# PSUM copies moved to ScalarE, a mask step moved to GpSimd, and a new order of TensorE's units in a four-layer graph network

## The chip, the cores and the metric

The kernel runs on one core of one Trainium2 chip. The metric is the device time of one execution in microseconds (us). Kernels are compared by the median of several executions, and a profile comes from one further execution, which has its own time. TensorE (PE in the profile) does the matrix products and the transposes, PEld is its loading of weights, VectorE is DVE, ScalarE is ACT, GpSimd is POOL, and SP issues the DMAs.

## What is computed

There are 32 graphs of 512 nodes with 256 features, each with a 512 by 512 adjacency matrix of zeros and ones. Four layers follow one another, each of them attention over the neighbours, and each ends in a sum with its own input and a layer norm:

```
x = norm(x + L0(x, adj))  # 4 heads of 64, relu, sum, norm per head
x = norm(x + L1(x, adj))  # one head, relu logits, elu
x = norm(x + L2(x, adj))  # 8 heads of 32, symmetric mask, then feed forward 1024
x = norm(x + L3(x, adj))  # one head, leaky relu logits
```

Layer 3 has logits f_i + g_j and, where they are negative, 0.2 times that; the softmax over the neighbours weighs the rows of h W. The kernel writes the numerator as max(exp(-0.8 f_i), exp(0.8 g_j)) times a factor exp(0.2 g_j), which is multiplied into the row j of the values, so that one vector instruction per tile makes the attention weights.

## The kernel before, in words

**Tiles.** A tile has 128 partitions; a graph has R = 4 row tiles and K = 2 column tiles. Every graph passes through ten steps: `edges` (the transposed adjacency is loaded in two halves and turned into bytes by ScalarE), `x`, `layer 0`, `layer 1`, `mask` (the adjacency is loaded and joined with its transpose, `symmetric`, line 378), `qkv`, `attention`, `projection`, `feed forward`, `layer 3`.

**Units and places.** Each step is a Python generator, cut by `yield` into units: for example `h0p` has one unit per row tile. `paced` (line 111) gives a unit a place, which is 12054 (`PERIOD`) times the graph's number plus a figure of the table `PLACES` (line 28). `heapq.merge` over the 32 graphs takes the unit with the lowest place next; where a unit's place lies below that of the unit just done, it follows at once. The order so made is TensorE's order, kept as it is (`manual_schedule`, line 798 and following). The instructions of the other engines are put in order by the tile framework, which lets ready instructions go ahead but mostly keeps the order in which they were written. So about four and a half graphs are under way together, and in the steady state each stretch of one period holds every unit once, of different graphs.

**Units by name.** The profile names TensorE's work by its result: h0p, gp, o (half tiles, `pt,hv`), den and backp for layer 0; xt1p, h1p, gp, o (`h,pt`) for layer 1; xt2p, qkp, vp for `qkv`; s, cp and den (`pr,ones`) for attention; wop for the projection; ytp, f1p, f2p for feed forward; xt3p, h3p, gp, o (`h,pt`) for layer 3. Line 104 is the helper that records all products. In this text gp0, gp1 and gp3 are the `gp` of the three layers, o0/2 is the unit of layer 0's product for j = 2 with its `den` matmuls, and s/c1j3h0 is a score unit of attention (half c, tile j, pair of heads h).

**Layer 0's products.** For each j of 4, VectorE makes four tiles `pt` (one per head, `kept`, line 394, instruction on line 397) out of `gb` (line 349), which TensorE multiplies in the unit o0/j. The `gb` and `pt` tiles, with others of the first layers, come from one ring of 9 buffers:

```python
        return buf([P, N], "part", name, {"a": 9, "c": 6}[stage[0]])
```

All four `gb` tiles are live until the last j, and `pt` tiles come free when the `den` matmuls of their j are done.

**The copies.** `evacuate` (line 304) gives a copy out of PSUM to VectorE for odd i and to ScalarE for even i; `transposed` (line 310) uses it for the two halves of each transposed matrix (xt1, xt2, xt3, yt), and layer 0 uses it for its three results `back`. `project` (line 323) copies each h tile by ScalarE. In layer 3 three exponentials (lines 711 to 713) then read all rows at once, and VectorE scales the values (line 714).

**The mask's diagonal.** `symmetric` takes the maximum of both directions on VectorE (line 388), sets the diagonal by a maximum with a small identity (line 390), and turns the last row tile into `shut` (line 391).

Of the kernel before, what the change touches and what calls it, by code (L numbers as in the profile page):

```python
# [14 lines left out]
ALU = mybir.AluOpType  # L15
# [10 lines left out]

PERIOD = 12054
PLACES = {
    "edges": [-5445, -1601, -916, 215],
    "x": [5461],  # L30
    "mask": [15415, 16243, 18300, 20727],
    "layer 0": [
        -31803, -31803, -30970, -28094, 618, 969, 969, 969, 8266, 10068, 10166, 10897,
        11770, 12293, 12293,
    ],
    "layer 1": [15146, 15174, 15397, 15397, 15397, 16015, 16537, 16946, 17233, 17233, 17233, 17233],
    "qkv": [19264, 19264, 22129, 22143, 22914, 23775, 24075, 24348, 24348, 24686, 25270],
    "attention": [
        -649, -498, -422, 1139, 26271, 26286, 26286, 26286, 26339, 26457, 26496, 27188,
        27431, 27452, 28958, 28958, 28979, 28979, 29061, 30394, 32151, 32151, 33609, 33609,  # L40
    ],
    "projection": [34273, 34335, 34335, 34355, 34984],
    "feed forward": [
        35875, 35881, 36402, 37091, 38264, 38376, 38376, 38428, 38428, 38589, 38589, 39322,
        39483, 39517, 39599, 40391, 41034, 41340, 41342,
    ],
    "layer 3": [44176, 44176, 45119, 45119, 45119, 46223, 46369, 47123, 47123, 47952, 47999, 48256],
}
STAGES = {"edges": "a", "x": "a", "layer 0": "a", "layer 1": "a", "feed forward": "c", "layer 3": "c"}
ALL = mybir.DependencyInfo(mybir.DependencyClass.Sync, mybir.DependencyReason.DATA)  # L50
# [22 lines left out]
def fast_path(ctx: ExitStack, tc: tile.TileContext, a: dict, out: bass.AP, bad: bass.AP):  # L73
# [230 lines left out]
    def evacuate(i, dst, src):  # L304
        if i % 2:
            nc.vector.tensor_copy(dst, src)
        else:
            nc.scalar.copy(dst, src)

    def transposed(y, name):  # L310

        t = buf([P, K, N], "xt", name, 1)
        for k in range(K):
            yield
            p = bank(name + "p")
            for r in range(R):
                product(nc.tensor.transpose,
                    p[:, r * P : (r + 1) * P], y[r][:, k * P : (k + 1) * P], ident
                )
            evacuate(k, t[:, k, :], p)  # L320
        return t

    def project(xt, w, cols, name):

        h = buf([P, R, cols], "h", name, {"a": 2}.get(stage[0], 1))
        for r in range(R):
            yield
            p = bank(name + "p")
            for k in range(K):
                product(nc.tensor.matmul,  # L330
                    p[:, :cols],
                    xt[:, k, r * P : (r + 1) * P],
                    w[:, k, :cols],
                    start=k == 0,
                    stop=k == K - 1,
                )
            nc.scalar.copy(h[:, r, :], p[:, :cols])
        return h
# [39 lines left out]
    def symmetric(b, at):  # L378

        a2 = sb.tile([P, R - 1, N], U8, tag="a2", name="a2", bufs=1)  # L380
        shut = sb.tile([P, N], BF16, tag="shut", name="shut", bufs=1)
        parts = [a2[:, r, :] for r in range(R - 1)] + [shut]
        for h in range(2):
            yield
            t = half(b, "adj", h)
            yield
            for r in range(h * R // 2, (h + 1) * R // 2):
                in_place(nc.vector.tensor_max(parts[r], at[:, r, :], t[:, r % (R // 2), :]))
                diag = parts[r][:, r * P : (r + 1) * P]
                nc.vector.tensor_max(diag, diag, identb)  # L390
        nc.vector.tensor_scalar(shut, shut, 0.0, SHUT, op0=ALU.is_equal, op1=ALU.mult)
        return a2, shut

# [7 lines left out]
    def layer0(x, xt, at, rd, mv, var):  # L401
        h = yield from project(xt, w0, D + 2 * H, "h0")
        values = hv[:, :, :, :HO]
        nc.vector.tensor_add(
            values,
            h[:, :, :D].rearrange("p r (h e) -> p r h e", h=H),
            bias0.rearrange("p (h e) -> p h e", h=H).unsqueeze(1).to_broadcast([P, R, H, HO]),
        )
        ex = buf([P, 2, H, R], "ex", "ex0", 2)
        s, d = h[:, :, D : D + H], h[:, :, D + H :]  # L410
        nc.scalar.activation(ex[:, 0], s.rearrange("p r h -> p h r"), AF.Exp, scale=-0.99)
        nc.scalar.activation(ex[:, 1], d.rearrange("p r h -> p h r"), AF.Exp, scale=0.99)
        nc.scalar.activation(hv[:, :, :, HO], d, AF.Exp, scale=0.01)
        nc.vector.tensor_mul(values, values, hv[:, :, :, HO:].to_broadcast([P, R, H, HO]))
        gbs = []
        for hh in range(H):
            gbs.append((yield from along(ex[:, 0, hh, :].unsqueeze(2), "gb0")))
        den, *ops = (bank(name) for name in ("den0", "o0", "o0"))
        for j in range(R):
            pt = [kept("pt0", gbs[hh], at[:, j, :], ex[:, 1, hh, j : j + 1]) for hh in range(H)]  # L420
            yield
            for hh in range(H):
                product(nc.tensor.matmul,
                    ops[hh // 2][hh % 2 * HO : (hh % 2 + 1) * HO, :],
                    hv[:, j, hh, :HO],
                    pt[hh],
                    start=j == 0,
                    stop=j == R - 1,
                )
            for hh in range(H):  # L430
                product(nc.tensor.matmul,
                    den[hh * DH : (hh + 1) * DH, :],
                    hv[:, j, hh, HC - DH :],
                    pt[hh],
                    start=j == 0,
                    stop=j == R - 1,
                )
        back = []
        for i, o in enumerate((den, *ops)):
            t = part("back")  # L440
            evacuate(i, t, o)
            back.append(t)
        y = sb.tile([P, R, D], F32, tag="y", name="y0", bufs=3)
        for i in range(1 + H // 2):
            yield
            p = bank("backp")
            for r in range(R):
                product(nc.tensor.transpose,
                    p[:, r * P : (r + 1) * P], back[i][:, r * P : (r + 1) * P], ident
                )  # L450
            if i == 0:
                rdh = rd.rearrange("p (i r h) -> p i r h", i=H // 2, r=R)
                for i in range(H // 2):
                    nc.vector.reciprocal(
                        rdh[:, i],
                        p.rearrange("p (r h e) -> p r h e", r=R, h=H)[
                            :, :, 2 * i : 2 * i + 2, DH - 1
                        ],
                    )
                continue  # L460
            nc.vector.scalar_tensor_tensor(
                y[:, :, (i - 1) * P : i * P].rearrange("p r (h e) -> p r h e", h=2),
                p.rearrange("p (r h e) -> p r h e", r=R, h=2),
                0.0,
                rdh[:, i - 1].unsqueeze(3).to_broadcast([P, R, 2, HO]),
                op0=ALU.max,
                op1=ALU.mult,
            )
        nc.vector.tensor_add(x, x, all_rows(bet0))
        nc.vector.tensor_add(y, y, h[:, :, :D])  # L470
        head_layernorm(y, 1e-6, var)
        nc.vector.tensor_mul(y, y, all_rows(gam0))
        nc.vector.tensor_add(y, y, x)
        layernorm(y, 1e-5, mv[0])
        return y
# [229 lines left out]

    def layer3(x, at, rd, mv):
        xt = yield from transposed([x[:, r, :] for r in range(R)], "xt3")
        h = yield from project(xt, w3g, D + 2, "h3")
        ex = buf([P, 2, R, 1], "ex", "ex3", 2)
        f, g = h[:, :, D : D + 1], h[:, :, D + 1 :]  # L710
        nc.scalar.activation(ex[:, 0], f, AF.Exp, scale=-0.8)
        nc.scalar.activation(ex[:, 1], g, AF.Exp, scale=0.8)
        nc.scalar.activation(f, g, AF.Exp, scale=0.2)
        nc.vector.tensor_mul(h[:, :, :D], h[:, :, :D], f.to_broadcast([P, R, D]))
        gb = yield from along(ex[:, 0], "gb3")
        pt = [kept("pt3", gb, at[:, j, :], ex[:, 1, j, :]) for j in range(R)]
        for r in range(R):
            p = yield from attend(pt, h, r, "o3")
            nc.vector.reciprocal(rd[:, r : r + 1], p[:, D : D + 1])
            nc.vector.scalar_tensor_tensor(  # L720
                x[:, r, :], p[:, :D], rd[:, r : r + 1], x[:, r, :], op0=ALU.mult, op1=ALU.add
            )
        layernorm(x, 1e-5, mv[5])
        return x
# [736 lines left out]
```

## Time and profile before

| | |
|---|---|
| median of 3 runs | 3603.0 us (3601.5 to 3603.07) |
| the profiled execution | 3604.45 us, of which 3602.7 us are its span (first to last instruction) |
| PE, PEld | 3460.6 us and 2344.0 us busy |
| DVE, ACT, POOL | 3036.6, 2083.5 and 5.2 us busy |
| granted TensorE clock, mean | 0.987 |

How to read it: a group line gives the source line, the engine, the instruction with output and input tiles, its count, busy time, the mean duration of one, and the idle time before it with what ended that. A timeline line gives the start in us from the span's start, the duration of a merged piece, and in brackets the idle time ahead of it. Busy time of PE overlaps for neighbouring matmuls, so lines of one group can sum to more than the page's busy time; where a matmul waits in the pipeline, its record gets longer. A windows line gives the stretch, its length, and the busy us and number of instructions of each engine in it.

### The profile page before, as it was taken

The page shows a single profiled execution, that of the slowest core. Times are in us where ns is not written, and L with a number is a line of the kernel's source. Part 1 is how long each engine was busy: PE and PEld are TensorE (multiplying, and loading weights), DVE is VectorE, ACT ScalarE, POOL GpSimd, SP SyncE. Part 2 cuts the span into 40 slices and gives each one's busy share as a digit, 9 for nine tenths or more (in the row PEclk, how much of TensorE's full clock was granted, in tenths as well). Part 3 has the DMA queues.
Part 4 walks back from the last instruction along what each step waited for, and adds up shares of the span by engine and source line. Part 5 has one row for each costly group of instructions (what it writes and reads, how often), then busy time and mean ns, then how long its engine had stood idle before and what let it go on. Part 6 is the DMA issues. An engine that isn't in the chain of part 4 may idle for free.

```text
span 3602.7 us, 48721 instructions
## 1 busy us (share of the span) xinstructions
PE 3460.6 (96%) x17224; PEld 2344.0 (65%) x17318; DVE 3036.6 (84%) x5498; ACT 2083.5 (58%) x4993; POOL 5.2 (0%) x43
## 2 busy tenths in 40 slices
PE   6899999999999999999999999999999999999986
PEld 3466666766666766666776666776666776666655
DVE  5779888889888889888888888888988888988763
ACT  3556656656656655656655556655656655655542
POOL 0000000000000000000000000000000000000000
PEclk8999999999999999999999999999999999999998
DMA  4333332334332234333234332233323233323120
GB/s 127 82 74 88 66 75 66 70 77 88 68 76 65 68 77 88 71 74 68 65 77 88 75 71 70 61 77 88 82 64 71 60 76 88 88 58 66 36 53 13
DMA packets 164027, 260.85 MB, mean 72 GB/s; under 512 B 20416, under 2 KB 56384, under 8 KB 163776
## 3 DMA queue, kind: packets, MB, share of 16 engines
q1 hardware_dynamic: 163776, 257.65, 32.5%
q8 instruction: 140, 2.29, 0.3%
q14 instruction: 111, 0.91, 0.1%
HBM read 106.57 MB, written 16.78 MB: 34 GB/s over the span
## 4 chain that ended last, share of the span: by engine, by line
PE 90%; ACT 5%; DVE 3%; issue 1%; DMA 0%; SPq 0%; DVEq 0%; ACTq 0%
PE o L104 19%; PE f2p L104 12%; PE f1p L104 12%; PE s L104 7%; PE cp L104 7%; PE qkp L104 6%; PE den L104 5%; PE h3p L104 3%; PE h1p L104 3%; PE wop L104 3%; PE h0p L104 3%; PE vp L104 3%; ACT y L280 2%; PE gp L104 1%; ACT gb L349 1%; PE backp L104 1%
## 5 line engine op out<-in xcount | busy, mean ns | idle before, releaser
L397 DVE SCALAR_TENSOR_TENSOR pt<-gb,ex,at 128x512 f32<-128x512 f32 x768 | 526.5, 750 | 198.5 <-ACT gb L349 158.0
L611 ACT ACTIVATE pr<-s 128x512 f32<-128x512 f32 x1024 | 551.2, 612 | 32.4 <-PE s L104 16.4
L614 DVE TENSOR_TENSOR pr<-pr,a 128x1024 f32<-128x1024 f32 x384 | 459.8, 1218 | 38.4 <-ACT pr L611 38.4
L104 PE MATMUL f2p<-wf,ft 128*128 128x256 f32 x2048 | 485.3, 380 | 6.7 <-ACT ft L684 6.6
L104 PE MATMUL f1p<-yt,wf 128*128 128x256 f32 x2048 | 484.0, 379 | 0.0
L641 DVE TENSOR_TENSOR pr<-pr 128x1024 f32<-128x1024 f32 x384 | 453.6, 1218 | 31.6 <-PE cp L104 28.1
L104 PE MATMUL o<-h,pt 128*128 128x257 f32 x2048 | 474.2, 384 | 3.2 <-DVE pt L397 3.2
L104 PEld LDWEIGHTS o<-h,pt 128*128 128x128 f32 x2048 | 386.9, 192 | 83.5 <-DVE mvs L274 23.5
L104 PEld LDWEIGHTS f2p<-wf,ft 128*128 128x128 f32 x2048 | 385.1, 190 | 63.5 <-ACT ft L684 11.4
L104 PEld LDWEIGHTS f1p<-yt,wf 128*128 128x128 f32 x2048 | 387.1, 190 | 52.1 <-DVE lo L537 0.3
L280 ACT ACTIVATE y<-y,rs 128x256 f32<-128x256 f32 x768 | 398.5, 597 | 14.8 <-DVE rs L276 14.8
L684 ACT ACTIVATE ft<-f1p,cols 128x256 f32<-128x256 f32 x512 | 215.1, 473 | 311.9 <-PE f1p L104 311.9
L104 PE MATMUL s<-qk 128*128 128x512 f32 x1024 | 367.7, 465 | 3.7 <-DMA qk<-lo 2.4
L273 DVE BATCH_NORM_STATS2 bn<-y 128x6 f32<-128x256 f32 x768 | 296.1, 411 | 4.4
L104 PE MATMUL cp<-pr,v 128*32 128x512 f32 x2048 | 269.4, 609 | 5.5 <-DVE pr L614 3.7
L104 PE MATMUL o<-pt,hv 128*64 128x512 f32 x1024 | 264.7, 612 | 4.6 <-DVE pt L397 4.6
L104 PEld LDWEIGHTS s<-qk 128*128 128x128 f32 x1024 | 187.5, 191 | 109.3 <-issue 77.9
L104 PE MATMUL qkp<-xt,wqkv 128*128 128x512 f32 x512 | 240.8, 603 | 0.0
L349 ACT COPY gb<-gp 128x512 f32<-128x512 f32 x192 | 110.5, 581 | 167.4 <-PE gp L104 167.4
L104 PEld LDWEIGHTS o<-pt,hv 128*64 128x64 f32 x1024 | 69.9, 137 | 159.6 <-issue 83.2
L536 ACT ACTIVATE hi<-qkp,cols 128x512 fp32r<-128x512 f32 x128 | 87.9, 686 | 138.5 <-PE qkp L104 138.5
L104 PEld LDWEIGHTS qkp<-xt,wqkv 128*128 128x128 f32 x512 | 94.9, 191 | 108.8 <-issue 103.7
(145 smaller groups left out, 4615.6 us busy)
## 6 DMA issues: line engine op xcount, KB each, us to landing
qk<-hi SPq DMA_DIRECT2D x512, 128.0 KB, 3.4
qk<-lo SPq DMA_DIRECT2D x512, 128.0 KB, 4.0
adjt<-in_adjt SPq DMA_DIRECT2D x64, 512.0 KB, 3.8
adj<-in_adj SPq DMA_DIRECT2D x64, 512.0 KB, 3.8
xt<-in_xt SPq DMA_DIRECT2D x32, 512.0 KB, 3.6
x<-in_x SPq DMA_DIRECT2D x32, 512.0 KB, 6.4
out<-y SPq DMA_DIRECT2D x32, 512.0 KB, 4.9
wf<-in_w1t SPq DMA_DIRECT2D x1, 1024.0 KB, 8.0
```

The source lines that it names most:

```text
L104: latest[0] = what(*args, **kwargs).ins.name
L273: nc.vector.bn_stats(st[:, r, :], y[:, r, :])
L280: nc.scalar.activation(y[:, r, :], y[:, r, :], AF.Identity, bias=rs[:, 1, r : r + 1], scale=rs[:, 0, r : r + 1],)
L349: nc.scalar.copy(g, p)
L397: nc.vector.scalar_tensor_tensor(t, g, f, edges, op0=ALU.max, op1=ALU.mult)
L536: nc.scalar.activation(hi, p, AF.Identity, bias=bias)
L611: nc.scalar.activation(t[:, i, :], s, AF.Exp, scale=QSCALE)
L614: nc.vector.tensor_mul(t, t, edges)
L641: nc.vector.tensor_add(t, t, u)
L684: nc.scalar.activation(ft[:, f, :], p[:, f, :], AF.Relu, bias=bf1[:, ff + f : ff + f + 1])
```

## The change

Five edits, with all places given anew.

1. `transposed` copies both halves by ScalarE.
2. Layer 0 copies all three `back` tiles by ScalarE.
3. The diagonal of the mask is set by GpSimd: a selection with a fill value, on bytes for three row tiles and on bf16 for the fourth.
4. Layer 3 no longer calls `project`: each h3p tile is followed by three exponentials on one column of PSUM and a ScalarE copy scaled by one of them; the vector multiplication of line 714 is gone.
5. The table `PLACES` is new; `PERIOD` is not.

```diff
 PLACES = {
-    "edges": [-5445, -1601, -916, 215],
-    "x": [5461],
-    "mask": [15415, 16243, 18300, 20727],
+    "edges": [-3978, -1691, -957, 174],
+    "x": [5375],
+    "mask": [15529, 15550, 17375, 20858],
     "layer 0": [
-        -31803, -31803, -30970, -28094, 618, 969, 969, 969, 8266, 10068, 10166, 10897,
-        11770, 12293, 12293,
+        -32810, -32810, -32810, -32129, 5406, 5406, 5406, 5452, 8379, 10181, 10354, 11030,
+        12979, 12979, 12979,
     ],
-    "layer 1": [15146, 15174, 15397, 15397, 15397, 16015, 16537, 16946, 17233, 17233, 17233, 17233],
-    "qkv": [19264, 19264, 22129, 22143, 22914, 23775, 24075, 24348, 24348, 24686, 25270],
+    "layer 1": [15397, 15397, 15551, 15551, 15637, 16368, 16395, 17082, 17350, 17359, 17359, 17361],
+    "qkv": [17440, 17444, 22256, 22270, 23119, 23902, 25371, 25371, 25371, 25371, 25371],
     "attention": [
-        -649, -498, -422, 1139, 26271, 26286, 26286, 26286, 26339, 26457, 26496, 27188,
-        27431, 27452, 28958, 28958, 28979, 28979, 29061, 30394, 32151, 32151, 33609, 33609,
+        -2905, -2905, -2905, -1865, 26410, 26425, 26425, 26425, 26478, 26596, 27423, 27447,
+        27455, 27460, 28382, 28382, 28780, 28780, 29468, 30180, 32292, 32292, 33750, 33750,
     ],
-    "projection": [34273, 34335, 34335, 34355, 34984],
+    "projection": [34383, 34383, 34383, 34383, 35158],
...
-    "layer 3": [44176, 44176, 45119, 45119, 45119, 46223, 46369, 47123, 47123, 47952, 47999, 48256],
+    "layer 3": [44306, 44306, 45121, 45121, 46359, 46359, 46477, 48020, 48020, 48023, 48398, 48528],
 }
...
-            evacuate(k, t[:, k, :], p)
+            nc.scalar.copy(t[:, k, :], p)
...
                 diag = parts[r][:, r * P : (r + 1) * P]
-                nc.vector.tensor_max(diag, diag, identb)
+                if r < R - 1:
+                    diag = diag.bitcast(mybir.dt.int8)
+                nc.gpsimd.affine_select(
+                    diag,
+                    diag,
+                    pattern=[[-1, P]],
+                    compare_op=ALU.not_equal,
+                    fill=1.0,
+                    base=0,
+                    channel_multiplier=1,
+                )
...
             t = part("back")
-            evacuate(i, t, o)
+            nc.scalar.copy(t, o)
...
-        h = yield from project(xt, w3g, D + 2, "h3")
+        h = buf([P, R, D + 2], "h", "h3", 1)
         ex = buf([P, 2, R, 1], "ex", "ex3", 2)
-        f, g = h[:, :, D : D + 1], h[:, :, D + 1 :]
-        nc.scalar.activation(ex[:, 0], f, AF.Exp, scale=-0.8)
-        nc.scalar.activation(ex[:, 1], g, AF.Exp, scale=0.8)
-        nc.scalar.activation(f, g, AF.Exp, scale=0.2)
-        nc.vector.tensor_mul(h[:, :, :D], h[:, :, :D], f.to_broadcast([P, R, D]))
+        for r in range(R):
+            yield
+            p = bank("h3p")
+            for k in range(K):
+                product(nc.tensor.matmul,
+                    p[:, : D + 2],
+                    xt[:, k, r * P : (r + 1) * P],
+                    w3g[:, k, :],
+                    start=k == 0,
+                    stop=k == K - 1,
+                )
+            f, g = p[:, D : D + 1], p[:, D + 1 : D + 2]
+            nc.scalar.activation(ex[:, 0, r, :], f, AF.Exp, scale=-0.8)
+            nc.scalar.activation(h[:, r, D : D + 1], g, AF.Exp, scale=0.2)
+            nc.scalar.activation(ex[:, 1, r, :], g, AF.Exp, scale=0.8)
+            nc.scalar.activation(h[:, r, :D], p[:, :D], AF.Copy, scale=h[:, r, D : D + 1])
```

The places sorted as `heapq.merge` does it give TensorE's order in one period of the steady state. From layer 0's first product to its last the two orders are, with the number of row tiles behind a cross where a unit comes several times in a row:

```
before: f2p (last), o1 x3, h0p x4, gp0 x4, s/c1j3h1, xt3p x2, cp/c1j3, o0/0,
        xt2p x2, h3p x3, den1, h3p, o0/1, qkp x2, wop, o0/2, gp3, wop x3, qkp, o0/3,
        o3 x2, qkp, ytp, backp, ytp, o3 x2, vp, backp x2, f1p, vp x3
after:  f2p (last), o1 x3, s/c1j3h0, h0p x4, gp0 x4, s/c1j3h1, xt3p x2, cp/c1j3, o0/0,
        xt2p x2, h3p x2, den1, o0/1, h3p x2, qkp x2, wop x4, gp3, o0/2, o0/3, qkp x2,
        o3 x2, ytp, o3, ytp, o3, f1p, backp x3, vp x4
```

Before, s/c1j3h0 stood ahead of the last f2p. Later in the period, the score units stand in other places between f1p and f2p, and gp1 comes after cp/c1j1 and den0 (before: ahead of them).

More of the change, by code (lines that the diff above doesn't have):

```diff
@@ L28 @@
 PLACES = {
-    "edges": [-5445, -1601, -916, 215],
-    "x": [5461],
-    "mask": [15415, 16243, 18300, 20727],
+    "edges": [-3978, -1691, -957, 174],
+    "x": [5375],
+    "mask": [15529, 15550, 17375, 20858],
     "layer 0": [
-        -31803, -31803, -30970, -28094, 618, 969, 969, 969, 8266, 10068, 10166, 10897,
-        11770, 12293, 12293,
-    ],
-    "layer 1": [15146, 15174, 15397, 15397, 15397, 16015, 16537, 16946, 17233, 17233, 17233, 17233],
-    "qkv": [19264, 19264, 22129, 22143, 22914, 23775, 24075, 24348, 24348, 24686, 25270],
+        -32810, -32810, -32810, -32129, 5406, 5406, 5406, 5452, 8379, 10181, 10354, 11030,
+        12979, 12979, 12979,
+    ],
+    "layer 1": [15397, 15397, 15551, 15551, 15637, 16368, 16395, 17082, 17350, 17359, 17359, 17361],
+    "qkv": [17440, 17444, 22256, 22270, 23119, 23902, 25371, 25371, 25371, 25371, 25371],
     "attention": [
-        -649, -498, -422, 1139, 26271, 26286, 26286, 26286, 26339, 26457, 26496, 27188,
-        27431, 27452, 28958, 28958, 28979, 28979, 29061, 30394, 32151, 32151, 33609, 33609,
+        -2905, -2905, -2905, -1865, 26410, 26425, 26425, 26425, 26478, 26596, 27423, 27447,
+        27455, 27460, 28382, 28382, 28780, 28780, 29468, 30180, 32292, 32292, 33750, 33750,
     ],
-    "projection": [34273, 34335, 34335, 34355, 34984],
+    "projection": [34383, 34383, 34383, 34383, 35158],
     "feed forward": [
-        35875, 35881, 36402, 37091, 38264, 38376, 38376, 38428, 38428, 38589, 38589, 39322,
-        39483, 39517, 39599, 40391, 41034, 41340, 41342,
+        35968, 36004, 36525, 37429, 38387, 38478, 38499, 38551, 38551, 38733, 38733, 39509,
+        39509, 39647, 39706, 40498, 41141, 41450, 41519,
     ],
-    "layer 3": [44176, 44176, 45119, 45119, 45119, 46223, 46369, 47123, 47123, 47952, 47999, 48256],
+    "layer 3": [44306, 44306, 45121, 45121, 46359, 46359, 46477, 48020, 48020, 48023, 48398, 48528],
 }
```

## The prediction, made before the changed kernel ran

> **What bounds the kernel now.** I read the busy times by stretch first. One period is 107.8 us long, so I cut the span into periods. Columns: stretch, length, then busy us and instructions of PE, PEld, DVE, ACT, POOL, then clock and DMA.
>
> ```profile
> 0.00:51.80 51.80, 26.15 (x108) 11.63 (x108) 28.68 (x43) 16.45 (x34) 1.82 (x11) 0.90 0.60 190
> 1560.90:1668.60 107.70, 106.30 (x539) 72.64 (x541) 94.38 (x171) 64.75 (x157) 0.10 (x1) 1.00 0.33 74
> 3501.10:3602.70 101.60, 71.44 (x294) 51.64 (x292) 39.34 (x102) 28.25 (x71) 0.00 (x0) 0.85 0.04 12
> ```
>
> In the steady state (27 such stretches, nearly alike) TensorE is busy for 106.3 of 107.7 us: it sets the period, and its order is written down. VectorE (94.4) and ScalarE (64.8) matter only where TensorE stands and waits for them. So next, who keeps TensorE waiting over ten periods (1500 to 2578 us): total, times, longest.
>
> ```profile
> PE gp L104 <- ACT ex L411: 7.3, 10, 0.7
> PE xt3p L104 <- ACT y L280: 6.7, 40, 0.2
> ```
>
> That is 1.4 us a period, but a waiting transpose also gets a longer record. So I read TensorE's timeline of one period.
>
> ```profile
> 1561.41 5.37 PE L104 MATMUL o<-h,pt 128*128 128x257 f32 x24
> 1566.63 3.72 PE L104 MATMUL h0p<-w,xt 128*128 128x264 f32 x16
> 1571.08 1.96 PE L104 MATMUL gp<-ident,ex 128*128 128x128 f32 x16 [0.73 <-ACT ex L411]
> 1572.79 0.93 PE L104 MATMUL s<-qk 128*128 128x512 f32 x2
> 1573.57 0.39 PE L104 MATMUL s<-shut,identb 128*128 128x512 bf16 x1
> 1574.15 0.33 PE L104 MATMUL xt3p<-ident,y 128*128 128x128 f32 x1 [0.19 <-ACT y L280]
> ...
> 1575.62 0.77 PE L104 MATMUL xt3p<-ident,y 128*128 128x128 f32 x5 [0.16 <-ACT y L280]
> 1576.31 2.08 PE L104 MATMUL cp<-pr,v 128*32 128x512 f32 x16
> 1578.33 2.21 PE L104 MATMUL o<-pt,hv 128*64 128x512 f32 x8
> 1580.47 1.06 PE L104 MATMUL den<-pt,hv 128*32 128x512 f32 x8
> 1581.47 1.09 PE L104 MATMUL xt2p<-ident,y 128*128 128x128 f32 x8
> ```
>
> From the wait ahead of xt3p (1573.96) to cp (1576.31) go 2.35 us; eight undisturbed transposes take 0.92 (xt2p to the h3p that starts at 1582.39). So xt3p loses **1.43 us a period**, gp0 0.73, and o0/0 another 0.27 (2.21 against 1.94 for o0/1 to o0/3). Little else is lost: 2.4 us a period is what better places could win at most, besides switches between tile shapes.
>
> Last, VectorE around o0/3. Its four `pt` tiles are made like this:
>
> ```profile
> 1595.49 0.75 DVE L397 SCALAR_TENSOR_TENSOR pt<-gb,ex,at 128x512 f32<-128x512 f32 x1
> 1597.48 4.73 DVE L397 SCALAR_TENSOR_TENSOR pt<-gb,ex,at 128x512 f32<-128x512 f32 x7 [1.24 <-PE den L104]
> ```
>
> One tile is made ahead, then VectorE stands 1.24 us until o0/2's den (ends 1597.47) gives buffers back: of 9, four hold gb and four hold the pt in use. Today wop, gp3 and a qkp unit lie between o0/2 and o0/3, so TensorE doesn't notice. The first graph shows it without such cover, its o0 units back to back and VectorE otherwise idle:
>
> ```profile
> 26.27 3.29 PE L104 MATMUL o<-pt,hv 128*64 128x512 f32 x8
> 29.49 1.06 PE L104 MATMUL den<-pt,hv 128*32 128x512 f32 x8
> 30.48 3.29 PE L104 MATMUL o<-pt,hv 128*64 128x512 f32 x8
> ```
>
> A unit takes 3.29 there instead of 1.94: **1.35 us** of waiting.
>
> **What the skill says.** (1) The Trainium skill, "TensorEngine Tiling (Array Packing)", Key Properties: changing the tiling mode drains TensorE. The trace agrees: in the chain of waits, two o1-like units take 3.67 us behind a den (column tiles) and 3.48 behind a transpose, so 0.19 for leaving a run of column tiles. (2) "PSUM — Partial Sum Buffer", Engine vs sequencer instructions: the queues of the other engines are strict FIFO. The 1.24 us above agree: pt3, ready or not, stood behind the waiting pt. (3) "ScalarE: Activation LUTs", What ACT_TABLE_LOAD costs: 186 ns plus 0.833 ns an element, 93 more for each pointer operand. For 128x512 that gives 612; the traced copies take 581 to 604. For a 256-wide activation with a pointer it gives 492; the trace has 472 (L508). (4) "SBUF — State Buffer", Who interferes with whom: a VectorE instruction with two SBUF inputs and a GpSimd one that reads SBUF block each other. In the loop before, GpSimd runs only one memset a graph, so this trace doesn't show it.
>
> **The change, part by part** (per graph, 32 graphs).
>
> *VectorE is relieved.* Gone are five copies (22.1 + 22.1 + 22.0 + 21.9 + 21.3 = 109.4 us), the multiplication L714 (39.3) and the diagonals L390 (26.7 + 7.2 = 33.9): 182.6 us, or 5.7 of 94.4 us a graph. None of this is TensorE time by itself. VectorE is busy without a gap from 1564.5 to 1597 us, and there it helps: two L390 lie ahead of the pt for o0/0, about 0.4 us (0.17 and 0.2 from start to start). That covers o0/0's 0.27: **-0.24**.
>
> *ScalarE is loaded.* Five copies at 585 ns: +2.9 us. The h3 tiles: four scaled copies at 472 (nearest row L508) instead of 369: +0.4. Twelve exponentials of one column instead of three: 195 ns each by L711, though neighbours start only 0.10 apart, so +0.9 to +1.8. Together +4.2 to +5.1 on 64.8, about 70 of 107.8. Between 1576 and 1592 us ScalarE had over 6 us idle; half goes. Where I cost these at nothing, cover is there: h3p needs both xt3 copies, which should end near 1581.2 against h3p's start near 1582.3; qkp needs xt2 copies 6 us later; wop needs the den1 chain (4 us) with 8 us between. The raw f3 and g3 columns are read from PSUM directly, so gp3 isn't later. Two places are tight: f2p follows its relu by only f1p and one score unit where six exponentials (0.53 apart) are queued ahead, because f2p no longer stands between them; and gp1 to o1 shrinks from 5.9 to about 2.7 us, while the copy gb and four pt need 3.4 for the last. o1 asks for its last pt 1.3 us after it starts, so it nearly fits. For both together I take **+0.15**, ends 0 and +0.6.
>
> *The diagonal on GpSimd.* Four selections of 128x128. The nearest row is the setup's select on f32, 292 ns; times on POOL are rough, so 0.1 to 1 us each, 0.4 to 4 us a graph on an idle engine. L391 on VectorE now waits for the last, and behind it stand L588 and the pt of o0/2, which have 4 and 6 us to spare; attention reads the mask about 30 us later. The adj buffer is released by L388, as before, so SP's queue (adjt waits there for it) is not held longer. By (4) a select may block a VectorE instruction or wait for it, at most its length. A gain can't come but for VectorE's freed time, counted above. **0**, up to +0.2.
>
> *The places.* Sorting them gives the order in the section on the change. Four things count. (a) s/c1j3h0 moves from ahead of f2p to behind the three o1, so the chain f2p, norm, norm, xt3p gets its length more. An o1 and it take 2.66 us (1664.83 to 1667.49), an o1 alone 1.74 (5.22 for three): 0.92. xt3p's wait shrinks by that, and could vanish (1.43) if ScalarE takes the norm ahead of the gb copies. But the exponentials of s/c1j3h1 then come later against cp/c1j3, so I take **-0.95**. The wait ahead of gp0 stays: h0p and gp0 are still neighbours. (b) Runs of column tiles per period: eight before (cp+o0/0, den1, o0/1, o0/2, o0/3, cp, cp, cp+den0); after six (den1+o0/1 and o0/2+o0/3 are joined): 2 x 0.19 = **-0.38**. (c) Joining o0/2 and o0/3 takes their cover away: wop, gp3 and qkp (2.76 + 0.65 + 1.9) now lie elsewhere. At least 1.35 as in the first graph. Further, gp3 now stands ahead of o0/2, so the four pt3 (0.66 apart, 2.75 us) are written ahead of o0/3's pt; they can start 0.65 us into o0/2 and end some 0.55 us after den. If the scheduler keeps that order the stall is 1.9. I take the middle: **+1.65**, ends 0.8 (two tiles made ahead; the first graph's last unit lost 0.69) and 2.4. (d) den1 and o0/1 come one h3p earlier behind o0/0; their sums and pt get through because of the 1.0 us that L390 and the xt3 copy leave: 0, up to +0.5. The qk transfers for s/c1j0h1 took 9.7 us after s/c0j3h0 and now have 12 instead of 14: 0.
>
> The rest of a period has the same units with the same matmuls: TensorE's work doesn't change.
>
> **Sum.** -0.24 + 0.15 - 0.95 - 0.38 + 1.65 = +0.23 us a period; 29 of the 31 steps from graph to graph are like this: +6.7. At the start and the end a graph runs nearly alone and pairs of copies no longer run side by side: 0.5 each for xt1 and xt3 and 0.5 for back: +1.5. So 8.2 on the profiled execution's 3604.45 (span 3602.7 and 1.75 around it) gives 3612.7. That execution lies 1.45 above the median of 3603.0, so the forecast is **3611 us**.
>
> **Rivals.** *The wait is won and not lost again (faster).* VectorE and ScalarE keep up: xt3p's wait vanishes (-1.43) and the scheduler puts o0/3's pt ahead of pt3 (+1.35). With -0.24 and -0.38: -0.70 x 29 = -20, +1.5: 3584. For it: 5.7 us of VectorE are freed just where it is dense. Against it: gp0's copies are in the same ScalarE queue. The sum turns where o0/3's stall is 1.42 (with the rest as I took it). Chance 0.31. *The two cancel.* That stall near 1.4, all within 0.25 us a period: 3604. Chance 0.22. *ScalarE becomes the bound between h0p and h3p.* The exponentials of s/c1j3h1, queued behind gb and norm, hold cp by 0.5; o0/3 loses 1.9 (0.25 more than in the sum); the tight places cost 0.35 (0.2 more): 0.23 + 0.95 = +1.18 a period, x 29 + 1.5 = +36: 3639. Chance 0.15. *The forecast*, 0.32. That an edit doesn't do what it says: the selection could wait long for VectorE's port, but 4 us a graph on an idle queue stay hidden.
>
> **Numbers.** 0.2% (7 us) is about what a measurement of this kernel can tell from no change. Slower 0.32 + 0.15 = 0.47, same 0.22, faster 0.31. The range reaches from a stall of 1.0 with xt3p's wait gone (-1.43 - 0.38 - 0.24 + 1.0 = -1.05 a period: 3574) to the third rival, 3639.
>
> **What would show it.** Waits of PE for pt L397 at o0/3, about 1.5 us a period, and its o unit near 3.3 to 3.8 instead of 1.94; VectorE near 88.7, ScalarE near 70 a period; xt3p's eight transposes at 1.4 instead of 2.35; gp0's 0.73 unchanged; POOL under 4 us a period. I am wrong if o0/3 doesn't wait (then the ring isn't the limit), or if a new wait of over 0.5 us a period stands at cp, o1, f2p or h3p.

## The result, and the profile after

The changed kernel takes **3579.52 us** (median of 4 runs, 3576.63 to 3580.88), the kernel before beside it 3603.03 (4 runs, 3601.5 to 3603.22): the ratio is 0.9935, 95% interval 0.9917 to 0.9952. The change made the kernel faster by 23.5 us; the forecast was 8 us slower. The profiled execution of after has a span of 3576.7 us, 26.0 less than before's.

First the busy times of the page of after, then its windows (columns as in the prediction: start, one period, end).

```profile
PE 3444.8 (96%) x17254; PEld 2336.7 (65%) x17318; DVE 2906.9 (81%) x5178; ACT 2229.5 (62%) x5441; POOL 70.8 (2%) x171
```

```profile
0.00:51.80 51.80, 26.08 (x108) 10.68 (x108) 27.70 (x41) 16.84 (x35) 1.83 (x11) 0.88 0.60 190
1560.00:1667.00 107.00, 105.88 (x538) 72.40 (x539) 90.06 (x162) 69.27 (x169) 2.10 (x5) 1.00 0.32 74
3475.10:3576.70 101.60, 71.83 (x298) 51.22 (x298) 36.33 (x97) 33.95 (x96) 0.00 (x0) 0.87 0.03 11
```

TensorE still sets the period. VectorE fell from 94.4 to 90.1 us in such a stretch, ScalarE rose from 64.8 to 69.3. In the last 101.6 us, too, work has gone from VectorE (39.3 to 36.3) to ScalarE (28.3 to 34.0). Who keeps TensorE waiting in after, over ten periods (1500 to 2570 us):

```profile
PE gp L104 <- ACT ex L421: 7.3, 10, 0.7
PE xt3p L104 <- ACT y L280: 3.2, 20, 0.2
```

gp0's 0.73 is unchanged, the waits of xt3p are halved, and there is **no wait for pt at o0/3**. TensorE's timeline of one period of after, from gp0 to cp/c1j3 and around o0/3:

```profile
1559.56 1.96 PE L104 MATMUL gp<-ident,ex 128*128 128x128 f32 x16 [0.73 <-ACT ex L421]
1561.28 0.47 PE L104 MATMUL s<-qk 128*128 128x512 f32 x1
...
1564.04 2.57 PE L104 MATMUL cp<-pr,v 128*32 128x512 f32 x16
...
1585.30 1.94 PE L104 MATMUL o<-pt,hv 128*64 128x512 f32 x8
1587.17 1.06 PE L104 MATMUL den<-pt,hv 128*32 128x512 f32 x8
1588.16 1.94 PE L104 MATMUL o<-pt,hv 128*64 128x512 f32 x8
1590.03 1.06 PE L104 MATMUL den<-pt,hv 128*32 128x512 f32 x8
```

o0/3 (1588.16) follows o0/2's den without a pause and takes 1.94 like the others. VectorE in the same stretch says why. Lines L407 are the pt tiles, L668 adds wop's result, L547 makes `lo`.

```profile
1576.25 3.40 DVE L407 SCALAR_TENSOR_TENSOR pt<-gb,ex,at 128x512 f32<-128x512 f32 x5
...
1579.68 0.75 DVE L407 SCALAR_TENSOR_TENSOR pt<-gb,ex,at 128x512 f32<-128x512 f32 x1
1580.52 0.75 DVE L547 SCALAR_TENSOR_TENSOR lo<-qkp,cols,hi 128x512 fp32r<-128x512 f32 x1
1581.19 0.74 DVE L407 SCALAR_TENSOR_TENSOR pt<-gb,ex,at 128x512 f32<-128x512 f32 x1
...
1582.90 0.76 DVE L668 TENSOR_TENSOR y<-wop,y 128x256 f32<-128x256 f32 x2
...
1585.44 0.72 DVE L407 SCALAR_TENSOR_TENSOR pt<-gb,ex,at 128x512 f32<-128x512 f32 x1
```

The first five are o0/2's four and o0/3's first; o0/3's second and third follow between the `lo` tiles, its fourth at 1585.44, just after o0/2 began (1585.30) and long before its den ends (1588.2). So all four were made *ahead*, where I counted one spare buffer. (The four tiles of gp3, the last L407 before 1590, begin at 1586.42, behind them.)

Where the 26.0 us of span went, by the start of the first matmul of h0p: the fifth comes 5.8 us earlier (380.82 before, 375.05 after); the next 27 periods are 107.27 instead of 107.81 long in the mean (most of them 107.24 to 107.25 and 107.80), 14.6 us in all; from there to the end it is 305.29 instead of 310.89, 5.6 us.

### The profile page after: what moved, and what is told of

Read it like the earlier page. It is cut to its first block, busy times and chain, and to the rows that moved or that the text cites. A ratio compares the mean times of both kernels' runs of the same rounds, so it can differ in the third digit from the quotient of the medians.

```text
span 3576.7 us, 49612 instructions
## 1 busy us (share of the span) xinstructions
PE 3444.8 (96%) x17254; PEld 2336.7 (65%) x17318; DVE 2906.9 (81%) x5178; ACT 2229.5 (62%) x5441; POOL 70.8 (2%) x171
## 4 chain that ended last, share of the span: by engine, by line
PE 83%; DVE 10%; ACT 6%; issue 1%; DMA 0%; SPq 0%; ACTq 0%; DVEq 0%
PE o L104 15%; PE f2p L104 13%; PE f1p L104 12%; PE cp L104 8%; PE qkp L104 6%; PE s L104 6%; PE den L104 5%; PE h1p L104 3%; PE h3p L104 3%; PE wop L104 3%; PE vp L104 3%; DVE bn L273 3%; ACT y L280 2%; PE backp L104 1%; DVE relu L520 1%; DVE y L710 1%
## 5 line engine op out<-in xcount | busy, mean ns | idle before, releaser
L407 DVE SCALAR_TENSOR_TENSOR pt<-gb,ex,at 128x512 f32<-128x512 f32 x768 | 534.8, 740 | 54.9 <-ACT gb L349 48.6
L621 ACT ACTIVATE pr<-s 128x512 f32<-128x512 f32 x1024 | 537.4, 612 | 36.4 <-PE s L104 30.6
L624 DVE TENSOR_TENSOR pr<-pr,a 128x1024 f32<-128x1024 f32 x384 | 452.6, 1219 | 45.6 <-ACT pr L621 43.2
L280 ACT ACTIVATE y<-y,rs 128x256 f32<-128x256 f32 x768 | 398.6, 593 | 29.4 <-DVE rs L276 29.1
L104 PE MATMUL s<-qk 128*128 128x512 f32 x1024 | 350.2, 458 | 4.4 <-DMA qk<-lo 2.1
L273 DVE BATCH_NORM_STATS2 bn<-y 128x6 f32<-128x256 f32 x768 | 298.2, 412 | 5.6
L104 PE MATMUL cp<-pr,v 128*32 128x512 f32 x2048 | 290.7, 607 | 2.6 <-ACT pr L621 1.1
L104 PE MATMUL o<-pt,hv 128*64 128x512 f32 x1024 | 256.9, 608 | 6.3 <-DVE pt L407 6.3
L104 PE MATMUL qkp<-xt,wqkv 128*128 128x512 f32 x512 | 233.5, 599 | 0.0
L547 DVE SCALAR_TENSOR_TENSOR lo<-qkp,cols,hi 128x512 fp32r<-128x512 f32 x128 | 95.7, 749 | 144.8 <-ACT hi L546 133.5
```

Source lines behind the costliest of these rows:

```text
L104: latest[0] = what(*args, **kwargs).ins.name
L273: nc.vector.bn_stats(st[:, r, :], y[:, r, :])
L280: nc.scalar.activation(y[:, r, :], y[:, r, :], AF.Identity, bias=rs[:, 1, r : r + 1], scale=rs[:, 0, r : r + 1],)
L407: nc.vector.scalar_tensor_tensor(t, g, f, edges, op0=ALU.max, op1=ALU.mult)
L547: nc.vector.scalar_tensor_tensor(lo, p, bias, hi.bitcast(F32), op0=ALU.add, op1=ALU.subtract)
L621: nc.scalar.activation(t[:, i, :], s, AF.Exp, scale=QSCALE)
```

## The experiments

The theory after the result has two parts. **The last reader:** o0/3 is the last of the four units that read gb. Each pt tile made for it is the last reader of its own gb and frees that buffer for the next tile, so one spare buffer is enough for all four. **VectorE's time:** the buffers alone don't help; VectorE must also come to these tiles before wop's sums, and the time for that is what the edits freed. The e10 run below keeps the first part and corrects the second: the place in VectorE's queue counts, and not its time. Rivals: the places alone bring the gain; the edits alone bring it; or the form of the work on ScalarE counts, not VectorE's time. Undone edits are measured against the changed kernel's period, 107.24.

I compare periods by units, in us from the start of one unit to the start of the next, in a period of the steady state (neighbouring periods of a trace differ by some hundredths of a us):

| kernel | xt3p | cp/c1j3 | o0/0 | o0/1 | o0/3 | cp/c0j1 | period |
|---|---|---|---|---|---|---|---|
| before | 2.16 | 2.02 | 2.14 | 1.87 | 1.87 | 2.02 | 107.80 |
| e2_edits (old places) | 2.17 | 2.01 | 1.95 | 1.87 | 1.87 | 2.19 | 107.80 |
| after | 1.76 | 2.50 | 1.87 | 1.87 | 1.87 | 2.36 | 107.24 |
| e1_places (no edits) | 1.27 | 5.06 | 1.87 | 1.87 | 3.90 | 3.23 | 112.27 |
| e5_gb_held | 1.76 | 2.50 | 1.87 | 1.86 | 3.84 | 2.61 | 109.46 |
| e6_copies_shared | 1.76 | 2.50 | 1.87 | 2.37 | 2.89 | 2.92 | 109.34 |
| e7_layer3_old | 1.75 | 2.50 | 1.87 | 1.86 | 3.42 | 2.62 | 109.06 |
| e10_layer3_pool | 1.76 | 2.50 | 1.87 | 1.86 | 1.87 | 2.35 | 107.24 |
| e8_diag_dve | 1.28 | 5.06 | 1.87 | 1.86 | 1.87 | 2.35 | 109.35 |

**Places and edits apart.** e1_places is the kernel before with the new `PLACES` alone, e2_edits the changed kernel with the old `PLACES`.

> The kernel before with only the new table of places; all five edits undone. Theory P (the order of TensorE's units makes the gain, and o0/3 needs no cover because in the last j every pt tile frees the gb tile that it reads): o0/3's unit stays at 1.94 us, no wait of PE for pt there, period near 107.3 instead of 107.8 us, time 3580 to 3590. Theory V (the 5.7 us a graph taken off VectorE let it make o0/3's tiles in time): with VectorE loaded as before, o0/3 waits 1.35 us or more a period, period 108.3 or more, time 3605 to 3625.

> The changed kernel with the old table of places; only the five edits. Theory P: TensorE's order is as before, so only o0/0's 0.27 us a period can be won: period 107.5 to 107.8, time 3595 to 3605. Theory V: VectorE's relief is what counts, most of the gain is here: period 107.3 or less, 3580 to 3590.

e1_places: 3727.45 us, 1.0342 of before (1.0327 to 1.0356). e2_edits: 3598.90, 0.9987 (0.9980 to 0.9994). So the places alone cost 124 us and the edits alone win 4.7; together they win 23.5. Neither carries the gain by itself. In e1 the stall that I forecast is there:

```profile
1538.62 1.07 PE L104 MATMUL o<-pt,hv 128*64 128x512 f32 x2
1540.19 2.40 PE L104 MATMUL o<-pt,hv 128*64 128x512 f32 x6 [0.51 <-DVE pt L397]
```

and VectorE made one tile of o0/3 ahead, as in before; the other three end the row of five that begins at 1538.06, behind the last two of gp3's tiles:

```profile
1531.64 0.74 DVE L397 SCALAR_TENSOR_TENSOR pt<-gb,ex,at 128x512 f32<-128x512 f32 x1
...
1538.06 3.40 DVE L397 SCALAR_TENSOR_TENSOR pt<-gb,ex,at 128x512 f32<-128x512 f32 x5
```

The unit takes 3.90 instead of 1.87: 2.03 us, between my 1.9 and my upper end of 2.4. Between those two lines VectorE had no pause over 0.32 us: wop's sums and two of gp3's tiles stand there in its queue. The larger loss of e1 is another, though: cp/c1j3 takes 5.06 instead of 2.02, to which e8 comes back.

**The ring.** Two kernels touch the buffers of the changed kernel. e3_ring8 has one fewer; e5_gb_held has four tiny VectorE maxima after o0/3 that read gb, whose results nothing uses, so that gb stays taken through o0/3.

```diff
-        return buf([P, N], "part", name, {"a": 9, "c": 6}[stage[0]])
+        return buf([P, N], "part", name, {"a": 8, "c": 6}[stage[0]])
```

> The changed kernel with 8 instead of 9 buffers in the first layers' ring, so that four gb and four pt fill it and no spare is left. Theory P: the chain of freed gb tiles can't begin before o0/2's den, all four pt of o0/3 come after it, 0.8 us before its first product and 0.7 for each further: o0/3's unit loses 2 us or more a period, 3630 to 3650. Theory V: the ring doesn't bind, 3578 to 3590.

```diff
             back.append(t)
+        for g in gbs:
+            nc.vector.tensor_max(late, g[:, :1], back[0][:, :1])
```

> The changed kernel with four more VectorE instructions a graph, each reading one column of a gb tile and of the first back tile, so that the gb tiles are live until after o0/3; nothing else. If freed gb tiles are what lets o0/3's pt tiles be made ahead (theory P), three of the four must now wait for o0/2's den, and o0/3 takes 3.3 to 3.8 us instead of 1.94: +1.35 to +1.9 us a period, 3620 to 3635. If VectorE's earliness alone does it (theory V), four instructions of about 0.16 us beside TensorE's work: 3578 to 3585.

e3_ring8: 3675.90, 1.0202 (1.0188 to 1.0216); TensorE waits for pt ten times in ten periods, 14.4 us in all, so all nine buffers are needed. e5_gb_held: 3646.83, 1.0120 (1.0104 to 1.0135). Its o0/3 looks like e1's:

```profile
1617.08 1.07 PE L104 MATMUL o<-pt,hv 128*64 128x512 f32 x2
1618.59 2.40 PE L104 MATMUL o<-pt,hv 128*64 128x512 f32 x6 [0.44 <-DVE pt L408]
```

Here VectorE had time: it stood 0.78 and 0.97 us. Where after makes o0/3's second and third tile, in e5 it stands:

```profile
1609.44 0.75 DVE L550 SCALAR_TENSOR_TENSOR lo<-qkp,cols,hi 128x512 fp32r<-128x512 f32 x1 [0.78 <-ACT hi L549]
1611.15 0.75 DVE L550 SCALAR_TENSOR_TENSOR lo<-qkp,cols,hi 128x512 fp32r<-128x512 f32 x1 [0.97 <-ACT hi L549]
```

With gb held the unit takes 3.84, with gb given back 1.87. 1.97 us of the period hang on the last reader's release. One thing this doesn't explain: in before, the second tile of o0/3 waited 1.24 us for o0/2's den, although the first had read its gb to the end by 1596.24. Who had taken that buffer isn't known.

**Each edit undone in the changed kernel.** e6_copies_shared goes back to `evacuate` for the transposes and `back`, e7_layer3_old to `project` with three exponentials and the vector multiplication, e8_diag_dve to the maximum with the identity.

```diff
-            nc.scalar.copy(t[:, k, :], p)
+            evacuate(k, t[:, k, :], p)
...
-            nc.scalar.copy(t, o)
+            evacuate(i, t, o)
```

> The changed kernel with the five copies a graph shared between VectorE and ScalarE again. Theory V (VectorE's time as such): 3.4 of its 5.7 us come back, so the larger part of what the places cost without the edits (148 us) returns: 3640 to 3680. Theory O (an edit matters by the order in which the instructions are queued, and brings a stall back whole or not at all): the copies stand behind o0/0 and o0/1, not ahead of cp/c1j3 or o0/3's tiles: 3575 to 3595.

```diff
-        h = buf([P, R, D + 2], "h", "h3", 1)
+        h = yield from project(xt, w3g, D + 2, "h3")
...
+        nc.vector.tensor_mul(h[:, :, :D], h[:, :, :D], f.to_broadcast([P, R, D]))
```

> The changed kernel with layer 3's values copied by one ScalarE copy each, three exponentials for all rows, and the multiplication by VectorE (1.2 us) again. Theory V: 1.2 of 5.7 us, 3600 to 3615. Theory O: the multiplication is queued between the tiles of o0/2 and o0/3, so o0/3's wait returns whole (2.0 us a period) and cp's doesn't: 3630 to 3645.

```diff
-                nc.gpsimd.affine_select(
...
+                nc.vector.tensor_max(diag, diag, identb)
```

> The changed kernel with the diagonal set by VectorE again. Theory V: 1.06 of 5.7 us, 3600 to 3615. Theory O: two of the four maxima are queued in the norms ahead of xt3p and cp/c1j3, so cp/c1j3's wait (2.1 us a period) returns whole and o0/3's doesn't: 3630 to 3645; if it is the copies that turn the order there, 3575 to 3590.

e6: 3642.08, 1.0107 (1.0090 to 1.0124). e7: 3634.37, 1.0087 (1.0070 to 1.0104). e8: 3637.60, 1.0098 (1.0081 to 1.0115). Each one undone makes the kernel slower than *before*, by 31 to 39 us. In e6 and e7 two tiles of o0/3 instead of three come ahead of wop's sums. In e6, VectorE stood 0.62 us between these two, waiting for ScalarE's `hi`, with the second tile behind that step in its queue. In e7, the multiplication L724 stands where the changed kernel makes the first of them:

```profile
1600.92 2.73 DVE L407 SCALAR_TENSOR_TENSOR pt<-gb,ex,at 128x512 f32<-128x512 f32 x4
1603.64 1.23 DVE L724 TENSOR_TENSOR h<-h 128x1024 f32<-128x1024 f32 x1
...
1605.85 0.74 DVE L407 SCALAR_TENSOR_TENSOR pt<-gb,ex,at 128x512 f32<-128x512 f32 x1
```

e8 loses elsewhere. o0/3 stays at 1.87, but cp/c1j3 takes 5.06 instead of 2.50, and the waits ahead of xt3p are gone (1.28). The order of ScalarE's queue has turned. First after, then e8 (L280 is a norm, L621 and L611 are exponentials of s/c1j3h1, which cp/c1j3 reads):

```profile
1561.21 2.08 ACT L280 ACTIVATE y<-y,rs 128x256 f32<-128x256 f32 x4
...
1564.33 0.60 ACT L621 ACTIVATE pr<-s 128x512 f32<-128x512 f32 x1
...
1564.90 0.61 ACT L621 ACTIVATE pr<-s 128x512 f32<-128x512 f32 x1
1565.40 2.08 ACT L280 ACTIVATE y<-y,rs 128x256 f32<-128x256 f32 x4
```

```profile
1586.97 2.08 ACT L280 ACTIVATE y<-y,rs 128x256 f32<-128x256 f32 x4
1588.95 1.05 ACT L611 ACTIVATE pr<-s 128x512 f32<-128x512 f32 x2
```

In after the exponentials stand ahead of the second norm, in e8 (and e1) behind it, and cp waits 1.7 us for them there (16.9 us in ten periods). Undoing a small VectorE instruction moved two ScalarE instructions by a norm's length, 2.1 us. That the order is set when the program is built, by when each is expected to be ready, is what I conclude; no run sets the order by itself. The times of e7 and e8 are those that I had expected if an edit counts by the order in the queues; that of e6 isn't.

**VectorE's time, or the form of the work?** e10_layer3_pool is e7 with the multiplication on GpSimd: layer 3 in its old form, but without its 1.23 us on VectorE.

```diff
-        nc.vector.tensor_mul(h[:, :, :D], h[:, :, :D], f.to_broadcast([P, R, D]))
+        nc.gpsimd.tensor_mul(h[:, :, :D], h[:, :, :D], f.to_broadcast([P, R, D]))
```

> e7_layer3_old with the multiplication given to GpSimd: ScalarE's part as before the change (one copy a tile, three exponentials a graph), VectorE free of the 1.2 us. If what cost e7_layer3_old its 55 us is VectorE's time ahead of o0/3's tiles, three of the four tiles are made ahead again, o0/3 takes 1.9 instead of 3.4 us, and the time is 3575 to 3585. If it is the form of ScalarE's work in layer 3, o0/3 stays at 3.4 us and the time at 3625 to 3640.

3581.26, 0.9939 (0.9922 to 0.9955): the changed kernel's time, its period and its o0/3 of 1.87. So the scaled copies aren't needed. But VectorE's time isn't what matters either. GpSimd, then VectorE in e10:

```profile
1580.01 2.33 POOL L724 TENSOR_TENSOR h<-h 128x1024 f32<-128x1024 f32 x1 [3.54 <-ACT h L723]
```

```profile
1577.18 3.40 DVE L407 SCALAR_TENSOR_TENSOR pt<-gb,ex,at 128x512 f32<-128x512 f32 x5
1580.49 1.88 DVE L806 SCALAR_TENSOR_TENSOR ok<-mvs,ok 128x20 f32<-128x20 f32 x1
1582.30 0.74 DVE L407 SCALAR_TENSOR_TENSOR pt<-gb,ex,at 128x512 f32<-128x512 f32 x1
```

The small instruction L806 takes 0.17 us in the changed kernel (there L817). Here it lasts until the multiplication on GpSimd ends, 1.88 us. So VectorE loses 1.71 us just ahead of o0/3's second tile, more than the 1.23 that it was spared, and over the whole run it is busy longer in e10 (2951.5 us) than in e7 (2934.4). Nothing comes of it: the second and third tile still stand ahead of wop's sums, as in the changed kernel, and the third ends at 1584.35, 4.7 us ahead of o0/3 (1589.09). In e7 the third stands behind wop's sums and behind gp3's tiles. What the edits win at o0/3 is thus a **place in VectorE's queue**, not time on it.

**The run of column tiles.** e11_o3_apart is the changed kernel with o0/3 behind one qkp unit (one place of layer 0 from 11030 to 11500), which opens one of the two joined runs again and changes little else.

> The changed kernel with one place altered: o0/3 comes behind the next qkp unit, so that o0/2 and o0/3 are two runs of column tiles again. If joining two runs saves what the chain of waits shows for leaving one, 0.19 us a period, the time is 3579.5 + 5.5: 3583 to 3588. If it saves nothing (the switch is hidden by the weight loads), 3577 to 3582. If o0/3 still lost something by its neighbourhood, the time falls below 3575.

3583.78, 0.9941 (0.9925 to 0.9958). The times of the runs overlap with the changed kernel's, but the period of the steady state in its trace is 107.44: **0.20 us** for one more run.

**gp0's wait.** e12_s_first moves s/c1j3h1 between h0p and gp0 to cover the 0.73 (one place of attention from 30180 to 29498).

> The changed kernel with one place altered: s/c1j3h1 stands between h0p and gp0, where TensorE waits 0.73 us for an exponential, instead of behind gp0. If the waits there are separate, gp0's 0.73 us vanish and cp/c1j3 gets its exponentials 1.7 us earlier (0.6 us), against up to 0.8 more at xt3p: 0 to -0.6 us a period, 3562 to 3580. If one chain through ScalarE's queue sets them all (exponentials ahead of the gb copies and of the norm), xt3p waits for all that gp0 saved and more: 3580 to 3600.

3625.93, 1.0062 (1.0045 to 1.0078). gp0's wait is gone, and o0/0 now waits for its tiles, 11.9 us in ten periods:

```profile
1588.59 3.06 PE L104 MATMUL o<-pt,hv 128*64 128x512 f32 x8 [1.19 <-DVE pt L407]
```

The exponentials now go ahead of the gb copies in ScalarE's queue (1581.70; the gb copies from 1584.62), xt3p has four waits again, and the period is 108.84. The wait that I called unchanged was a cheap one.

**A guess that didn't hold.** e9_places_sq tested another owner for the spare buffer in e1: the squares of the adjacency take a buffer of the same ring, so here they are written over the adjacency tile.

```diff
-            squares = part("squares").bitcast(BF16).rearrange("p (r n) -> p r n", n=N)
-            nc.scalar.activation(squares, t, AF.Square, accum_out=sums[:, 1, i : i + 1])
+            nc.scalar.activation(t, t, AF.Square, accum_out=sums[:, 1, i : i + 1])
```

> The kernel before with the new places (e1_places), and the squares of the adjacency written over the adjacency tile, so that they take no buffer of the ring. In e1_places only one tile of o0/3 was made before o0/2's den. If the squares took the buffer of the first freed gb (theory S), the tiles are now made ahead and o0/3 loses its 2.0 us of waiting: period 110.2, 3660 to 3675. If VectorE came too late anyway (theory V), 3715 to 3730.

3863.69, 1.0718 (1.0700 to 1.0736). o0/3 stays at 3.90, so the squares don't hold it up. cp/c0j1 grew from 3.23 to between 6.7 and 7.6 us, with waits of 2.5 us for a `pr` tile of VectorE. Its queue has turned: steps of layer 0's norm (L300, L302) stand between the four tiles that cp reads, and the fourth begins 4.4 us after cp. Why it turned isn't settled.

## Why the prediction was wrong, step by step

**The step that failed is (c) of the places**: "At least 1.35 as in the first graph", taken as +1.65. It measured 0. Two errors lie in it. First, I counted nine buffers (four gb, four pt, one spare) and forgot that for the last j the reader of gb frees it (in before one tile did wait for den all the same, as said above). The 1.35 came from j = 1 and 2, whose gb is still needed; the same graph's last unit lost 0.69, and I kept that only as an end (0.8). e5 shows the release is worth 1.97. Second, I took it that "the four pt3 are written ahead of o0/3's pt", an order right with the instructions of before: e1 has it, with 2.03. With the edits it is wrong: all four tiles of o0/3 stand ahead of gp3's. e7 (+1.55), e6 (+1.02) and e10 (0) show that it hangs on what else stands in VectorE's queue. I priced the relief of VectorE once, as time at o0/0, and didn't ask how it changes the order in the queue. The first rival had this order ("the scheduler puts o0/3's pt ahead of pt3"). The pause of 1.24 us, by the way, doesn't show what (2) of the prediction reads from it: gp3 began only at 1597.39, so pt3 couldn't have run in it.

The other terms, per period:

- *VectorE relieved*, -0.24: o0/0 went from 2.14 to 1.87, **-0.27**; in e2, without the places, only -0.19. VectorE's busy time fell by 129.7 us, 4.1 a graph, not 5.7: I added durations, and neighbours overlap (copies are 0.69 long and 0.60 apart); counted without overlap, the instructions that went hold 139 us of before's VectorE time. Its stretch without a gap, too, ended at 1596.24 and not at 1597.
- *ScalarE loaded*, "about 70": 69.3. The scaled copy is 0.47, as taken.
- *Tight places*, +0.15: no wait at f2p, and none at o1 in the steady state. *The diagonal on GpSimd*, 0: hidden, at 2.1 us a period. But undoing it alone costs 2.1 us a period (e8), through ScalarE's order and not through GpSimd. My 0 was right only as a cost.
- *(a)*, -0.95: from the start of s/c1j3h1 to cp it was 3.52 (1572.79 to 1576.31), now 2.76 (1561.28 to 1564.04): **-0.76**. But cp/c1j3 got **+0.48**, since its last exponential ends at 1565.5, 1.5 after cp began. That is the third rival's step ("hold cp by 0.5"), which I had left out of the sum. cp/c0j1 lost another **+0.34**, which I did not foresee. It waits for VectorE: the last of the four multiplications of pr by the mask, right behind a step of layer 0's norm (L295), ends 1.32 us after cp begins (1615.59, 1614.27), in before 0.97 (1627.64, 1626.67). The transposes backp, which that norm needs, now end 8.7 instead of 9.5 us ahead of cp. Why e2 has 0.17 of it with the old places is open.
- *(b)*, -0.38: e11 measures 0.20 for one of the two runs; taken for both, **-0.40**. *(d)*, 0: o0/1 unchanged at 1.87. gp0's 0.73: unchanged.

These sum to -0.27 - 0.76 + 0.48 + 0.34 - 0.40 = -0.61, against -0.56 measured (-0.54 in the mean of 27); the forecast was +0.23. Had (c) been 0, my sum would have been -1.42. So the other terms together promised 0.8 too much, most of which is what the two cp gave back (+0.82), and that hid part of the error in (c).

**Start and end**, +1.5: measured -11.4 with the steps there counted in, where steps like the others would give some -2. At the start nearly all of it is one step, from the third h0p to the fourth (109.34 before, 104.00 after): 2.3 us from the first qkp to the first ytp (181.54 to 206.27 before, 180.87 to 203.34 after), where before splits wop around an o0 unit and two o0 units take 2.5 and 3.0; 1.8 from the next cp to xt1p (220.24 to 240.74, 216.66 to 235.39), where before's f2p waits 0.90. At the end, the way from the last h0p to the first of three long waits for xt3p is 2.8 us shorter (117.11 and 114.33), that from the second to the third 2.2 (74.40 and 72.18). I had costed the pairs of copies alone and not looked at the places there. The other traces, one each, tell the parts apart in some measure. The step from the third h0p to the fourth is 109.2 in e2 and 106.0 in e1, so most of it is the places; it is 107.3 and 107.2 in e6 and e7 but 104.0 and 103.9 in e10 and e8. From the last h0p to the end, e1 (313.33) and e2 (311.95) have no gain over before: there neither brings it alone. Where e2 wins its 4.7 us isn't known, since its profiled execution took 3603.24, 4.3 above its median.

The first rival (3584) was nearest, and its turning point, a stall of 1.42, was the right question. It was right about o0/3 and wrong about xt3p, whose wait didn't vanish.

## What to carry to other kernels

Before pricing a stall on a ring of buffers, ask for each unit who reads the shared buffer last: the last round frees as it goes, and a stall measured in an earlier round doesn't carry over. Then look where the instructions that fill the ring stand in their engine's queue: a free buffer and an early place are two conditions, and here neither was enough without the other. An edit that takes an instruction away may count by the order it leaves behind and not by its time: e10 lost more of VectorE's time than it spared, and kept the whole gain at o0/3. Price an order and the edits that come with it together, and test them apart: here -4.7 and +124 make -23.5.

## What I had not expected of the hardware

A selection of 128x128 bytes on GpSimd took 582 ns in the mean (96 of them), one on bf16 308 ns, and a multiplication of 128x1024 f32 2291 ns, where VectorE takes 1.23 us. The multiplication's length cost nothing in e10, since o3 begins some 15 us after the last h3 tile (the last scaled copy at 1578.35, o3 at 1594.56 in after). Single selections took 0.29 us beside VectorE instructions with one input (L273) and 0.69 to 0.72 beside those with two (L388, L522), which had begun before them and kept their 0.66 to 0.69. In e10 it was VectorE that stood: its L806, begun 0.48 us after GpSimd's multiplication, took 1.88 instead of 0.17 us. So both sides of the mutual blocking that the prediction quoted from the Trainium skill ("SBUF — State Buffer", Who interferes with whom) were seen here, each time on the engine that began later. An activation of one column from PSUM takes 165 to 180 ns, but neighbours start 50 to 150 ns apart, so three of them cost ScalarE 0.26 us ahead of the copy.
